# A recurrence split into two stages: RWKV block and cross-attention on one core

## Chip, core, metric

One core of a Trainium2 chip. The metric is the device time of one execution in microseconds (us); the time of a kernel is the median of its runs.

## What is computed

Sixteen sequences x[b] (128 tokens, 512 channels) and as many contexts ctx[b] go through two layers in fp32. The first is an RWKV block: a layer norm, interpolation of each token with the one before it, five mixed inputs, from them r, k, v, gate g and a per-channel decay w, a recurrence over time on 32 heads of 16x16 state, a group norm, an output projection and a gated feed-forward. The state comes from rows of ctx. The second is a cross-attention of the result with the same context.

```python
xa = _ln(x, ln1_w, ln1_b)
sx = concatenate([state[:, 1:2] - xa[:, :1], xa[:, :-1] - xa[:, 1:]], axis=1)
xxx = tanh((xa + sx * maa_x) @ maa_w1).reshape(b, l, 5, DM)
xm = xa[:, :, None] + sx[:, :, None] * (maa_stack + einsum('blfd,fde->blfe', xxx, maa_w2))
xk, xw, xv, xr, xg = (xm[:, :, j] for j in range(5))
w = exp(-exp(time_decay + tanh(xw @ td_w1) @ td_w2))
r, k, v, g = xr @ Wr.T, xk @ Wk.T, xv @ Wv.T, silu(xg @ Wg.T)
def step(s, r_t, k_t, v_t, w_t):            # scanned over 128 tokens
    a = k_t[..., :, None] * v_t[..., None, :]
    out = einsum('bhi,bhij->bhj', r_t, u * a + s)
    return a + w_t[..., :, None] * s, out
...
x1 = x + groupnorm(out) * g @ Wo.T
xc = _ln(x1, ln2_w, ln2_b)
x2 = x1 + sigmoid(xr2 @ Wfr.T) * (square(relu(xk2 @ Wfk.T)) @ Wfv.T)
...
A = softmax(conv(Wn, inorm(x2)).T @ conv(Wm, inorm(ctx)))
return conv(Wo, conv(Wl, ctx) @ A.T) + x2
```

## The kernel before

The sixteen sequences are worked in eight groups g of n = 2 sequences b. A group passes through Python generators, each of which yields after every piece of its work:

- stageB: layer norm and transposes (norm_T, xaT), the shift sx, the product p1 with maa_w1, tanh, and the stacked operand sk (lines 222 to 257).
- stageB2: five interpolations px, xm in the order 0, 3, 1, 2, 4, one ahead of its use; from them k, r, w, v and the gate, in five pieces. v and the gate go to DRAM (vD, gD). w is ready after the third piece.
- stageR: the recurrence, in chunks of 32 tokens. For each sequence, pair products over blocks of four tokens are laid out in PP (L374) from ru = u*r (L371), summed over a head by matmuls with emat into pq (L385), transposed (L390) and put into the attention matrix AM (L392). Then three levels (blocks of 4, 8 and 16 tokens): k is scaled by running decays in place (L416), copied to ks (L401), spread block-diagonally into KX by eight DMAs on SP's queue (L405), multiplied with r (pl, L435) and put into AM (L437). Last, for each sequence: k transposed to kt (L457), the state carried over three chunks (pu L479, Sn, Sx), AM transposed to at (L493), and the output po (L500, L505), its variance and the group norm of y (L524).
- stageC: y transposed (py, L545), gate, Wo (ptk, L559), second layer norm, feed-forward Wfk (L586), Wfr, Wfv.
- stageL: the cross-attention of the group (pn, pS, pA, pO, lines 663 to 688); stageX loads what it needs of the context (MV), which stageE computed earlier into DRAM.

Of the eight PSUM banks bx and c have two each, pt, lv, ls and la one each. A tile waits until its buffer (same tag) is free. The recurrence uses lv (pq, pl, pu, po) and pt (p4, pk, pa); pt also serves the transposes of both layer norms and of y. One buffer each: wl, ru and at (one tag), kt, y, PP, AM, KX, w; two each: k, r, vt, xaT, sx, and the stacked operand stk[g % 2].

A loop over steps sets the order. In a step, stage k of group step - OFF[k] is live (B 0, B2 1, R 2, C 3, L and X 4), and interleave takes the next piece of the stage with the least DLY + share done; NEED says which stage of the same group must be over. EARLY gives the groups whose contexts are computed in steps 0 to 2 as extra work. That order is a priority: when the program is built, a scheduler fills each engine's queue with the instruction of highest priority whose operands and buffers are free in its own model of time. On the chip each queue then runs in order. All loads are issued on SP's queue.

Of the kernel before, what the change touches and what calls it, by code (L numbers as in the profile page):

```python
# [7 lines left out]
FP = mybir.dt.float32  # L8
# [10 lines left out]
n = 2  # L19
# [7 lines left out]
OFF = [0, 1, 2, 3, 4, 4]  # L27
ORDER = [3, 4, 2, 1, 0, 5]
DLY = [-0.2, 0.2, 0.0, 0.4, 0.8, 0.4]
EARLY = {0: [0, 1], 1: [2, 3], 2: [4, 5, 6, 7]}  # L30
LASTX = 2
# [3 lines left out]
def rwkv_xattn_kernel(ctx: ExitStack, tc: tile.TileContext, a: dict, out: bass.AP):  # L35
# [9 lines left out]
    PSB = dict(bx=2, c=2, pt=1, lv=1, ls=1, la=1)  # L45
# [55 lines left out]
    stk = [const.tile([98, 5, 256], FPR, name=f"sk{i}") for i in range(2)]  # L101


    KX = const.tile([128, 4 * n, 8, 64], FP, name="KX")
# [4 lines left out]
    def clear():  # L109
        for sk in stk:  # L110
            nc.gpsimd.memset(sk[96:98].bitcast(FP), 1.0)
        nc.gpsimd.memset(PP.rearrange("p a f -> p (a f)"), 0.0)
        nc.gpsimd.memset(KX.rearrange("p a h s -> p (a h s)"), 0.0)
        nc.gpsimd.memset(VX.rearrange("p c q f -> p (c q f)"), 0.0)
        nc.gpsimd.memset(AM.rearrange("p b h s -> p (b h s)"), 0.0)
# [72 lines left out]
    def norm_T(xs, sidx, vw, vb, g, xT, how, ssum):  # L188
# [7 lines left out]
        for c0 in range(0, 4, 2):  # L196
            pt = ps.tile([128, 2, n, 128], FP, name="pt", **T("pt"))
# [24 lines left out]
    def stageB(g):  # L222
# [3 lines left out]
        xaT = sb.tile([128, 4, n, 129], FP, name="xaT")  # L226
        norm_T(x, 1, V_LN1W, V_LN1B, g, xaT, "dve", (None, None))
        yield
        sx = sb.tile([128, 4, n, 128], FP, name="sx")
# [14 lines left out]
        th = sb.tile([128, 2, NT], FP, name="th", tag="xn")  # L244
# [4 lines left out]
        sk = stk[g % 2]  # L249
# [10 lines left out]
    def stageB2(g):  # L260
        d = D[g]
        xaT, sx, sk = d["xaT"], d["sx"], stk[g % 2]
# [85 lines left out]
    def stageR(g):  # L348
        d = D[g]
        k, r, w, vt = d["k"], d["r"], d["w"], d["vt"]  # L350

        wl = sb1.tile([128, 4 * n, 124], FP, name="wl")
        src = w.rearrange("p c b t -> p (c b) t")
        for m in PRO:
            v = src.rearrange("p a (k s) -> p a k s", s=2)
            dst = wl[:, :, WOFF[2 * m] : WOFF[2 * m] + 64 // m]
            nc.vector.tensor_tensor(dst, v[:, :, :, 0], v[:, :, :, 1], ALU.mult)
            src = dst
        kf, rf = (t.rearrange("p c b t -> p (c b) t") for t in (k, r))
        s0 = sb1.tile([128, n, 4, 16], FP, name="s0")  # L360
        nc.sync.dma_start(out=s0.rearrange("p b c j -> p (b c j)"), in_=a["s0"][g])
        sm = small.tile([128, n, 4], FP, name="sm")
        nc.vector.tensor_reduce(sm, s0, AX.X, ALU.add)
        nc.vector.tensor_scalar(sm, sm, 1.0 / S, None, ALU.mult)
        nc.vector.tensor_tensor(s0, s0, sm[:, :, :, None].to_broadcast([128, n, 4, 16]), ALU.subtract)
# [3 lines left out]
        ru = sb1.tile([128, 4, n, 128], FP, name="ru", tag="at")  # L369
        for cc in range(4):  # L370
            nc.scalar.activation(ru[:, cc], r[:, cc], AF.Identity, scale=vec[:, V_U, cc : cc + 1])  # L371

        def pairs(b):
            tt = lambda o, x, y: nc.vector.tensor_tensor(o, x, y, ALU.mult)  # L374
            tt(dg[:, :, :, 0:128:4], four(ru, b, 0, 4), four(k, b, 0, 4))
# [7 lines left out]
            pq = ps.tile([128, 512], FP, name="pq", **T("lv"))  # L383
            for cc in range(4):
                nc.tensor.matmul(pq[32 * cc : 32 * cc + 32], lhsT=emat, rhs=PP[:, cc, 0:512], start=True, stop=True)  # L385
            pc = sb1.tile([128, 512], FP, name="pc4", tag="kt")
            nc.scalar.copy(pc, pq)
            p4 = ps.tile([128, 4, 4, 32], FP, name="p4", **T("pt"))
# [8 lines left out]
        def expand(li):  # L397

            m = LEV[li]
            ks = sb1.tile([128, 4 * n, 64], FP, name="ks", tag="sq")  # L400
            nc.scalar.copy(ks.rearrange("p a (q m) -> p a q m", m=m),  # L401
                           kf.rearrange("p a (q s m) -> p a q s m", s=2, m=m)[:, :, :, 0])
            for h in range(8):
                p = slice(16 * h, 16 * h + 16)
                nc.sync.dma_start(out=KX[p, :, h], in_=ks[p])  # L405

# [10 lines left out]

        for b in range(n):
            pairs(b)
            yield  # L420
        decay(kf, 1, 0)
        decay(kf, 2, 0)
        expand(0)
        decay(kf, 4, 0)
        decay(rf, 1, 1)
        decay(rf, 2, 1)
        yield
        for li, m in enumerate(LEV):
            pl = []
            for b in range(n):  # L430
                t = ps.tile([128, 512], FP, name="pl", **T("lv"))
                for cc in range(4):
                    for c in range(4):
                        cs = slice(32 * c, 32 * c + 32)
                        nc.tensor.matmul(t[cs, 128 * cc : 128 * cc + 128], lhsT=r[:, cc, b, cs],  # L435
                                         rhs=KX[:, n * cc + b, :, 16 * c : 16 * c + 16], start=True, stop=True)
                nc.vector.copy_predicated(  # L437
                    AM[:, b].rearrange("p h (q s m) -> p h q s m", s=2, m=m)[:, :, :, 0],
                    lvm[:, li].rearrange("p (q m) -> p q m", m=m)[:, None].to_broadcast([128, 32, 16 // m, m]),
                    t.rearrange("p (h q m) -> p h q m", h=32, m=m))  # L440
                yield
            decay(rf, m, 1)
            if li < 2:
                expand(li + 1)
                decay(kf, 2 * m, 0)
            yield
        y = sb1.tile([128, n, 512], FP, name="y")
        var = small.tile([128, n, 32], FP, name="var", bufs=2)
        for b in range(n):
# [4 lines left out]

            pk = ps.tile([128, 512], FP, name="pk", **T("pt"))
            for cc in range(4):
                nc.tensor.transpose(pk[:, 128 * cc : 128 * cc + 128], k[:, cc, b], ident)  # L457
            kt = sb1.tile([128, 512], FP, name="kt")
            nc.scalar.copy(kt, pk)

# [10 lines left out]
            vb = vt[:, b].rearrange("p (q x j) -> p x q j", q=4, x=8)  # L471
            yield
            for c in range(3):
                cs = slice(32 * c, 32 * c + 32)
                pu = ps.tile([128, 4, 4, 16], FP, name="pu", **T("lv"))
                for cc in range(4):
                    for hf in range(2):
                        f = slice(64 * hf, 64 * hf + 64)
                        nc.tensor.matmul(pu[f, cc], lhsT=kt[cs, 128 * cc + 64 * hf : 128 * cc + 64 * hf + 64],  # L479
                                         rhs=vb[cs, 2 * cc + hf], start=True, stop=True)  # L480
                wc = wl.rearrange("p (c b) s -> p c b s", b=n)[:, :, b, WOFF[32] + c]
# [6 lines left out]

            at = sb1.tile([128, 8, 128], FP, name="at")
            for x4 in range(2):  # L490
                pa = ps.tile([128, 4, 128], FP, name="pa", **T("pt"))
                for x in range(4):
                    nc.tensor.transpose(pa[:, x], AM[:, b, 4 * (4 * x4 + x) : 4 * (4 * x4 + x) + 4].rearrange("p h s -> p (h s)"), ident)  # L493
                nc.scalar.copy(at[:, 4 * x4 : 4 * x4 + 4], pa)
            yield
            po = ps.tile([128, 512], FP, name="po", **T("lv"))
            for cc in range(4):
# [4 lines left out]
                for x in (2 * cc, 2 * cc + 1):  # L502
                    for c in range(4):
                        cs = slice(32 * c, 32 * c + 32)
                        nc.tensor.matmul(po[cs, 64 * x : 64 * x + 64], lhsT=at[:, x, cs],  # L505
# [23 lines left out]
    def behind(g):  # L529

        return tc.issue_after(D[g]["last"].ins) if g < G else nullcontext()

    def stageC(g):
        d = D[g]
        with behind(g + 1):
# [6 lines left out]
        for b in range(n):  # L542
            pt = ps.tile([128, 4, 128], FP, name="py", **T("pt"))
# [30 lines left out]
        norm_T(x, 0, V_LN2W, V_LN2B, g, xcT, "act", ssum)  # L574
# [70 lines left out]
    def stageX(g):  # L645
        d = D[g]
        d["MV"] = []
        for b in range(n):
# [4 lines left out]
            with behind(g + 2):  # L653
# [4 lines left out]
    def stageLb(g, b):  # L658
# [5 lines left out]
        pn = ps.tile([128, 512], FP, name="pn", **T("ls", g, ("pt", "bx")[b]))  # L664
# [3 lines left out]
        for tt in range(4):  # L668
            tsl = slice(128 * tt, 128 * tt + 128)
            pS = ps.tile([128, 512], FP, name="pS", **T("ls", g, ("c", "lv")[b]))  # L670
# [135 lines left out]
```

## Time and profile before

| | |
|---|---|
| runs | 1028.33, 1029.72, 1031.13 us; median 1029.72 |
| profiled execution | 1028.91 us, span 1027.1 us |
| mean granted TensorE clock | 0.978 |
| busy | PE 933.8, PE weight loads 633.5, DVE 650.3, ACT 499.8, POOL 66.8 us |
| DMA | 128.7 MB on SP's queue, 41.3% of 16 engines; 33698 of 76461 packets under 512 B |

The page names engines PE (TensorE; PEld its weight loads, which overlap), DVE (VectorE), ACT (ScalarE), POOL (GpSimd) and SP (the queue that issues DMAs). The time of the execution includes 1.8 us around the span. In a line of the timeline or of groups, "out<-in" are tiles, the bracket gives idle time of that engine just before, and what ended it. L12 is line 12 of the kernel before.

### The profile page before, as it was taken

The numbers are of one execution on the slowest core, as the hardware profiler recorded it, in microseconds if no ns is written. First come the engines' busy times: TensorE is split into PE (matmuls) and PEld (weight loads), VectorE is DVE, ScalarE is ACT, GpSimd is POOL, SyncE is SP. The second block draws the span as 40 slices with busy tenths as digits, with TensorE's granted clock in tenths as the row PEclk, the third lists the DMA queues.
The fourth block names the chain that finished last, engine by engine and source line by source line (L and its number), as shares of the span: only waits on it lengthen the run. The fifth ranks groups of instructions, "written<-read, shape, count | busy, mean of one in ns | idle before, by whom it ended". The sixth has DMA issues, their size and how long they took to land.

```text
span 1027.1 us, 19266 instructions
## 1 busy us (share of the span) xinstructions
PE 933.8 (91%) x7588; PEld 633.5 (62%) x7588; DVE 650.3 (63%) x1569; ACT 499.8 (49%) x1017; POOL 66.8 (6%) x92
## 2 busy tenths in 40 slices
PE   4699899769998999999999999899999997897997
PEld 2565766546755586666765685657766664573655
DVE  6777766764757574874686485766594658463423
ACT  2565451253336543574446444464344555534645
POOL 5111000000000000000100000000000000000000
PEclk9899998889998999999999999999999999998999
DMA  5765646314641334515551435414454334262210
GB/s 158 246 219 190 192 134 198 97 26 140 225 134 21 108 122 145 168 18 155 177 176 38 128 112 165 138 32 145 144 174 120 90 127 138 39 193 64 77 57 32
DMA packets 76461, 129.91 MB, mean 126 GB/s; under 512 B 33698, under 2 KB 43426, under 8 KB 76369
## 3 DMA queue, kind: packets, MB, share of 16 engines
q1 hardware_dynamic: 76370, 128.68, 41.3%
q8 instruction: 60, 0.98, 0.4%
q14 instruction: 31, 0.25, 0.1%
HBM read 100.32 MB, written 22.04 MB: 119 GB/s over the span
## 4 chain that ended last, share of the span: by engine, by line
PE 65%; DVE 11%; ACT 9%; DMA 7%; SPq 4%; issue 2%; POOL 0%; ACTq 0%; DVEq 0%; POOLq 0%
PE ptk L559 15%; PE pj L219 13%; PE pj L586 5%; PE pv L321 5%; PE pO L685 4%; PE pS L671 4%; SPq L405 3%; PE pl L435 3%; PE pu L479 3%; PE p L241 2%; DVE PP L374 2%; PE pa L493 2%; DMA KX<-ks 2%; PE po L500 2%; PE pA L680 2%
## 5 line engine op out<-in xcount | busy, mean ns | idle before, releaser
L219 PE MATMUL pj<-xm,wb 128*128 128x256 f32 x768 | 182.7, 388 | 8.4 <-DVE xm L281 4.1
L219 PEld LDWEIGHTS pj<-xm,wb 128*128 128x128 f32 x768 | 145.2, 195 | 36.5 <-issue 8.2
L138 POOL TENSOR_TENSOR rs<-rs,mhalf 128x1 f32<-128x1 f32 x64 | 48.0, 754 | 586.0 <-DVE rs L123 509.7
L685 PEld LDWEIGHTS pO<-AT,MV 128*128 128x128 f32 x448 | 57.2, 191 | 18.5 <-issue 7.8
L671 PE MATMUL pS<-MV,Mn 128*128 128x512 f32 x112 | 59.8, 616 | 6.6 <-ACT e L675 3.7
L685 PE MATMUL pO<-AT,MV 128*128 128x128 f32 x448 | 62.3, 279 | 3.8 <-ACT AT L682 3.8
L281 DVE TENSOR_TENSOR xm<-px,sx 128x512 f32<-128x512 f32 x80 | 54.5, 686 | 14.7 <-PE px L278 14.5
L559 PE MATMUL ptk<-wb,yT 128*128 128x512 f32 x128 | 58.4, 610 | 2.3 <-issue 2.3
L673 DVE TENSOR_REDUCE nm<-pS 128x1 f32<-128x512 f32 x64 | 43.9, 690 | 25.6 <-PE pS L671 25.3
L559 PE MATMUL ptk<-wb,sx 128*128 128x512 f32 x128 | 58.9, 601 | 0.4 <-DMA wb<-in_Wfr_dram 0.3
L435 PE MATMUL pl<-KX,r 128*32 128x128 f32 x1536 | 53.5, 279 | 6.1 <-DMA KX<-ks 5.2
L586 PE MATMUL pj<-xk,wb 128*128 128x256 f32 x256 | 58.2, 380 | 0.3 <-DVE xk L145 0.3
L321 PE MATMUL pv<-wb,xm 128*128 128x512 f32 x128 | 57.5, 594 | 0.1
L559 PE MATMUL ptk<-wb,kk 128*128 128x512 f32 x128 | 57.5, 598 | 0.0
L675 ACT ACTIVATE e<-pS,nm 128x512 f32<-128x512 f32 x64 | 44.9, 701 | 23.5 <-DVE nm L673 23.5
L677 ACT ACTIVATE e<-e,nm 128x512 f32<-128x512 f32 x64 | 46.2, 725 | 19.2 <-DVE nm L676 19.0
L435 PEld LDWEIGHTS pl<-KX,r 128*32 128x32 f32 x1536 | 40.0, 111 | 23.8 <-issue 11.5
L282 DVE TENSOR_TENSOR xm<-xm,xaT 128x512 f32<-128x512 f32 x80 | 54.3, 687 | 0.5
L586 PEld LDWEIGHTS pj<-xk,wb 128*128 128x128 f32 x256 | 47.4, 190 | 6.5 <-DVE xk L145 0.6
L278 PE MATMUL px<-sk,w2s 98*128 98x256 f32 x160 | 42.9, 354 | 7.3 <-ACT w L302 4.9
L437 DVE COPY_PREDICATED AM<-lvm,pl 128x512 f32<-128x512 int32 x48 | 33.8, 705 | 23.4 <-PE pl L435 23.0
L682 ACT COPY AT<-pA 128x512 f32<-128x512 f32 x64 | 37.8, 590 | 19.7 <-PE pA L680 16.8
(160 smaller groups left out, 1685.8 us busy)
## 6 DMA issues: line engine op xcount, KB each, us to landing
mvD<-MVe SPq DMA_DIRECT2D x16, 512.0 KB, 3.8
wb<-in_Wk_dram SPq DMA_DIRECT2D x16, 512.0 KB, 3.5
wb<-in_Wr_dram SPq DMA_DIRECT2D x16, 512.0 KB, 3.9
wb<-wvc SPq DMA_DIRECT2D x16, 512.0 KB, 3.5
wb<-in_Wg_dram SPq DMA_DIRECT2D x16, 512.0 KB, 4.8
wb<-in_Wo_dram SPq DMA_DIRECT2D x16, 512.0 KB, 3.7
wb<-in_Wfk_dram SPq DMA_DIRECT2D x16, 512.0 KB, 4.3
wb<-in_Wfr_dram SPq DMA_DIRECT2D x16, 512.0 KB, 3.8
```

What stands on the lines that cost most here:

```text
L138: D["pow"] = nc.gpsimd.tensor_tensor(rs, rs, mhalf[:, 0:1], ALU.pow).ins
L219: nc.tensor.matmul(pj[:, m], lhsT=wb[:, m, cc, :], rhs=xm[:, cc], start=cc == 0, stop=cc == 3)
L281: nc.vector.tensor_tensor(xm[:, sl], px.rearrange("p c (b t) -> p c b t", b=n), sx[:, sl], ALU.mult)
L282: nc.vector.tensor_tensor(xm[:, sl], xm[:, sl], xaT[:, sl, :, 1:129], ALU.add)
L321: nc.tensor.matmul(pv, lhsT=xm[:, m, b], rhs=wbs[m // 2][:, m % 2], start=m == 0, stop=m == 3)
L435: nc.tensor.matmul(t[cs, 128 * cc : 128 * cc + 128], lhsT=r[:, cc, b, cs], rhs=KX[:, n * cc + b, :, 16 * c : 16 * c + 16], start=True, sto ...
L559: nc.tensor.matmul(pt, lhsT=act[:, m, b], rhs=wbs[m // 2][:, m % 2], start=m == 0, stop=m == 3)
L586: nc.tensor.matmul(pj[:, m], lhsT=wb[:, m, cc, :], rhs=xk2[:, cc], start=cc == 0, stop=cc == 3)
L671: nc.tensor.matmul(pS, lhsT=Mn[:, tsl], rhs=Mm, start=True, stop=True)
L675: nc.scalar.activation(e, pS, AF.Exp, bias=nm[:, 0:1], accum_out=nm[:, 1:2])
L677: nc.scalar.activation(e, e, AF.Identity, scale=nm[:, 2:3])
L685: nc.tensor.matmul(pO, lhsT=Vc[:, sc], rhs=AT[:, sc], start=sc == 0, stop=sc == 3)
```

## The change

stageR becomes stageR1 (pairs, levels, kt and at for both sequences) and stageR2 (state, po, y). R1 has a PSUM bank r1, R2 a bank r2; pt and lv are gone, B's layer-norm transposes use bx, C's use c. kt, at and w32 (the decays that R2 reads) are results of their own. R1 of a group becomes live in the step of its B2 and starts after B2's third piece; R2 and C follow in the next step, L one step later, so a group spans four steps instead of five. WHEN holds, for each stage, step offset, start, length and number of pieces. xaT, sx and the stacked operand have one buffer instead of two. ru is gone: u is applied in place on PP by ACT. KX is laid out with the head outside, and ks is made ahead (expand) of the copies into KX (place).

```diff
-OFF = [0, 1, 2, 3, 4, 4]
-ORDER = [3, 4, 2, 1, 0, 5]
-DLY = [-0.2, 0.2, 0.0, 0.4, 0.8, 0.4]
-EARLY = {0: [0, 1], 1: [2, 3], 2: [4, 5, 6, 7]}
+WHEN = {
+    B_: (0, 0.85, 0.3, 3),
+    B2_: (1, 0.2, 1.0, 5),
+    R1_: (1, 0.75, 0.7, 14),
+    R2_: (2, 0.0, 0.7, 14),
+    C_: (2, 0.8, 1.0, 5),
+    L_: (3, 0.3, 1.0, 6),
+    X_: (3, -0.1, 0.2, 2),
+}
+EARLY = {0: [0, 1], 1: [2, 3, 4], 2: [5, 6, 7]}
...
-    PSB = dict(bx=2, c=2, pt=1, lv=1, ls=1, la=1)
+    PSB = dict(bx=2, c=2, r1=1, r2=1, ls=1, la=1)
...
-    stk = [const.tile([98, 5, 256], FPR, name=f"sk{i}") for i in range(2)]
-    KX = const.tile([128, 4 * n, 8, 64], FP, name="KX")
+    sk = const.tile([98, 5, 256], FPR, name="sk")
+    KX = const.tile([128, 8, 4 * n, 64], FP, name="KX")
...
-            pt = ps.tile([128, 2, n, 128], FP, name="pt", **T("pt"))
+            pt = ps.tile([128, 2, n, 128], FP, name="pt", **T(bank))
...
-        xaT = sb.tile([128, 4, n, 129], FP, name="xaT")
+        xaT = sb1.tile([128, 4, n, 129], FP, name="xaT")
-        sx = sb.tile([128, 4, n, 128], FP, name="sx")
+        sx = sb1.tile([128, 4, n, 128], FP, name="sx")
...
-        ru = sb1.tile([128, 4, n, 128], FP, name="ru", tag="at")
-        for cc in range(4):
-            nc.scalar.activation(ru[:, cc], r[:, cc], AF.Identity, scale=vec[:, V_U, cc : cc + 1])
...
-            tt(dg[:, :, :, 0:128:4], four(ru, b, 0, 4), four(k, b, 0, 4))
+            tt(dg[:, :, :, 0:128:4], four(r, b, 0, 4), four(k, b, 0, 4))
+            for cc in range(4):
+                q = dg[:, cc, :, 0:128:4]
+                nc.scalar.activation(q, q, AF.Identity, scale=vec[:, V_U, cc : cc + 1])
...
-            ks = sb1.tile([128, 4 * n, 64], FP, name="ks", tag="sq")
+            ks = sb.tile([128, 4 * n, 64], FP, name="ks", tag="ks")
...
+        def place(ks):
             for h in range(8):
                 p = slice(16 * h, 16 * h + 16)
-                nc.sync.dma_start(out=KX[p, :, h], in_=ks[p])
+                nc.sync.dma_start(out=KX[p, h], in_=ks[p])
...
+        place(expand(0))
+        decay(kf, 4, 0)
+        k1 = expand(1)
...
+        for b in range(n):
+            level(0, b)
+            yield
+        place(k1)
+        decay(rf, 4, 1)
+        k2 = expand(2)
...
+        kt = d["kt"] = sb1.tile([128, n, 512], FP, name="kt")
+        for b in range(n):
+            pk = ps.tile([128, 512], FP, name="pk", **T("r1"))
...
+        at = d["at"] = sb1.tile([128, n, 8, 128], FP, name="at")
...
+    def stageR2(g):
+        d = D[g]
+        r, kt, at, w32 = d["r"], d["kt"], d["at"], d["w32"]
...
-                pu = ps.tile([128, 4, 4, 16], FP, name="pu", **T("lv"))
+                pu = ps.tile([128, 4, 4, 16], FP, name="pu", **T("r2"))
...
-            po = ps.tile([128, 512], FP, name="po", **T("lv"))
+            po = ps.tile([128, 512], FP, name="po", **T("r2"))
...
-            pt = ps.tile([128, 4, 128], FP, name="py", **T("pt"))
+            pt = ps.tile([128, 4, 128], FP, name="py", **T("c"))
...
+    NEED = {B_: (), B2_: (B_,), R1_: (), R2_: (R1_, B2_), C_: (R2_,), L_: (C_, X_), X_: (), E_: ()}
+    def ready(k, g):
+        return all((q, g) in done for q in NEED[k]) and (k != R1_ or count.get((B2_, g), 0) >= 3)
```

## The prediction

> **What bounds the kernel now.** I read the page first: busy time and chain.
>
> ```profile
> PE 933.8 (91%) x7588; PEld 633.5 (62%) x7588; DVE 650.3 (63%) x1569; ACT 499.8 (49%) x1017; POOL 66.8 (6%) x92
> ...
> PE 65%; DVE 11%; ACT 9%; DMA 7%; SPq 4%; issue 2%; POOL 0%; ACTq 0%; DVEq 0%; POOLq 0%
> ```
>
> TensorE is the bound, with 1027.1 - 933.8 = 93.3 us without a matmul. The change neither removes nor adds a matmul, so all it can touch is where those 93.3 us lie. The view by windows, cut where the stages of the pipeline change, says where (first number after the window: its length; then PE busy):
>
> ```profile
> 0.00:80.00 80.00, 54.77 (x262) 39.99 (x262) 54.02 (x150) 40.93 (x79) 24.64 (x30) 0.94 0.65 209
> 80.00:230.00 150.00, 127.56 (x1135) 91.55 (x1136) 102.82 (x231) 61.40 (x129) 6.99 (x11) 0.94 0.46 138
> 230.00:776.00 546.00, 527.30 (x4447) 358.95 (x4446) 369.09 (x873) 268.91 (x554) 26.59 (x37) 0.99 0.42 127
> 776.00:935.00 159.00, 147.49 (x1419) 95.81 (x1417) 91.91 (x227) 76.77 (x153) 4.87 (x8) 1.00 0.41 117
> 935.00:1027.10 92.10, 76.70 (x328) 47.16 (x328) 32.51 (x91) 51.76 (x106) 3.67 (x6) 0.96 0.16 52
> ```
>
> PE's idle time is 25.2 us in the first 80 (loading, before any recurrence), 22.4 to 230 (pipeline filling), 18.7 to 776 (five steady steps, 96.6% busy), 11.5 to 935 and 15.4 to the end (draining). So the steady part has 3.4% to give, and the fill and the drain the rest.
>
> Third view, the timeline round the hand-over from group 1's recurrence to group 2's, to see what holds it:
>
> ```profile
> 285.62 0.68 PE L479 MATMUL pu<-vt,kt 32*64 32x64 f32 x16
> ...
> 294.02 0.41 PE L505 MATMUL po<-VX,at 128*32 128x64 f32 x16
> 295.23 1.71 ACT L371 ACTIVATE ru<-r,vec 128x256 f32<-128x256 f32 x4
> 297.06 1.13 DVE L374 TENSOR_TENSOR PP<-ru,k 128x512 f32<-128x512 f32 x1
> 302.30 1.07 PE L385 MATMUL pq<-PP,emat 128*32 128x512 f32 x8
> 310.59 1.93 PE L385 MATMUL pq<-PP,emat 128*32 128x512 f32 x8 [4.26 <-DVE PP L374]
> ```
>
> ru shares at's buffer, so ru(2) waits for the last po(1) at 294.4, although r, k and w of group 2 exist; and PE then waits 4.26 us for the pair products. The same stands at 202.02 in the fill (4.86 us for PP), at 205.6 (1.6 us, a transpose of L200 waiting for AM L392: one bank, pt) and at 224.10 (1.45 us, py waiting for the copy of kt: pt again). From pq to the last po the one recurrence takes 194.7 to 294.4, then 302.3 to 405, 412.8 to 514: 100 to 103 us of a period of 110 to 115 (first Wo matmuls at 349.4, 459.7, 572.6, 687.3). It is a serial chain nearly as long as the period, and in the fill (C of group 0 can't start before y at 196, and starts at 224) it is longer than what PE has beside it.
>
> **The change, part by part.** The profiled run is 1028.9 us (span 1027.1 and 1.8 round it), 0.8 below the median 1029.7; I count from it.
>
> *Two stages, own banks and results.* R1 (pairs, three levels, kt, at) of a group no longer waits for the group before: its buffers are free once that group's R1 is over, kt and at excepted, which R2 must have read. R2's chain is short: in the drain pu(7) starts at 900.0, po of the first sequence ends at 907.3, y is scaled at 937.5, 38 us with C(6) beside. Fill: of the 22.4 us, I can name 11.8 as waits in R's own chain (1.95 at 104, 0.71+4.86+0.75+1.62+0.46 from 196 to 209, 1.45 at 222); beyond these, C(0), 32 us of matmuls, comes a step earlier, into the thin stretch 195 to 230. I take 14 and leave 8, the rate at which 135 to 175 idles now. Steady: of 18.7 I take 6 (4.26 and the 0.77 at 257.8 are R's, the rest is spread over exponentials, loads and softmax waits, which stay). Drain to 935: of 11.5 I take 4 (KX and PP waits of 1.27, 0.82 and 1.10 us, and something for the rest of R). End: y(7) and C(7) come earlier, while C(6) and L(6) still have work; of 15.4 I take 5, the waits of 2.79 and 2.28 us for y and yT. L(7) alone, from 996, keeps its 7 us. Sum: 14+6+4+5 = 29. Bounds: 12 (only the waits named outright in the fill) to 44 (everything after 80 us at the 1% idle of a quiet stretch, 855 x 1% = 9 left, plus the 15.4 at the end: 93 - 25 - 9 - 15).
>
> *Pair products scaled in place.* Four ru activations a group go, eight on strided quarters come, between the first product and pq.
>
> ```profile
> L371 ACT ACTIVATE ru<-r,vec 128x256 f32<-128x256 f32 x32 | 13.8, 501 | 0.1
> L547 ACT ACTIVATE yT<-py,vec 128x128 f32<-128x128 f32 x64 | 24.5, 489 | 7.1 <-PE py L545 7.1
> L374 DVE TENSOR_TENSOR PP<-ru,k 128x512 f32<-128x512 f32 x16 | 17.8, 1112 | 12.4 <-ACT ru L371 9.2 <-PE pq L385 3.3
> ```
>
> From below 0.28 us each (dt, 128x128, 278 ns); from above 0.79 (0.489 times 1112/690, what the stride of four costs on DVE). I take 0.49, the row of that shape with a scale: 8 x 0.49 - 4 x 0.50 = +1.9 us of ACT per group, hidden under ACT's 51% idle. In the chain it is 2.0 us per sequence, under the other five products (2.9 us of DVE) if those don't wait for it. Uncovered it shows for group 0 and group 7 alone: -2 (ru's 1.7 us ahead of the chain are gone) to +8; I take +2.
>
> *KX turned, so that a head's rows are 2 KB in one piece.* A train of eight copies stands before each level:
>
> ```profile
> KX<-ks SPq DMA_DIRECT2D x192, 32.0 KB, 2.2
> ...
> L405 SPq DMA_DIRECT2D KX<-ks x192: 585/598/1193, 99.4 to 886.8; - x192
> ...
> L654 SPq DMA_DIRECT2D MV<-mvD x14: 320/327/707, 256.9 to 904.9; - x14
> ```
>
> Issue: 598 ns against 327 for a plain two-dimensional copy: 8 x 0.27 = 2.2 us a level, 6.5 a group; landing 2.2, at best the 1.9 of s0's load (64 KB in 512 B pieces). On the path only where R1 leads (groups 0 and 7): 0 to -14, inside the 29. The moving operand now steps 2 KB between heads; no row shows it. I take nothing, with -0 to +0.3 us for each 1.08 us level (48 of them, +14) as bounds. [...] The row of s0, in pieces of 512 B, allows no more than 0.3 us a level.
>
> *Moved or shared.* B's transposes go from pt to bx (24 uses per group of two banks where 22 were), C's to c (12 for 8). Each such use is held for two transposes' worth and its evacuation, 1 to 2 us; PE is in order, so a late bank stops all matmuls behind it. 0 to 4 us in all, I take 1. R1 puts all 16 fills on one bank, pq(b=1) now behind the AM copies of b=0 (1.45 us); DVE's next products take 4 us anyway: nothing. place() waits on SP for the level before to be read; Wfv, Wo and MV loads queue behind it, as they do now (88.8 us of SP waits on pl): nothing. EARLY moves one group's context from step 2 to step 1: the same 37 us of filler.
>
> *xaT, sx and sk single.* B(g+1) may write only when B2(g) has its last xm. From the last xm to the next px there are now 18.7, 16.3, 21.5, 23.9, 28.7, 22.8 and 23.2 us; from the first xaT to the last sk of a group 14.7 to 17.8 us from group 3 on, 25 and 32 in the fill. It fits, narrowly. The new wait falls on an ACT instruction (L203) and a DVE one (sx); behind them on those queues stand the evacuations of pj, pS and pA, and PE waits for these. 0 to +8, I take +1 with the fill's other work as cover; the price without cover is the first rival.
>
> Sum: 1028.9 - 29 + 2 + 1 + 1 = 1003.9, so **1004 us**.
>
> [...]
>
> **The rivals.** *The B loop becomes the bound (slower).* B2 spreads its interpolations over 87.5 us in a steady step (256.0 to 343.5). If B's chain, now strictly behind it, takes the 32 us it once took (110.2 to 142.1), the loop is 119.5 against 112: 5 steps x 7.5 = 37, less 21 gained at both ends: 1045. It decides from a B chain of 24.5 us. Against: B2 has been done in 45 us (107.4 to 152.7), so it can be squeezed. Chance 0.20.
> *They don't run beside each other.* R1(g+1) starts only after B2's third piece, when w is there (343.5 for group 3); if R2 is then over, what is left is the freed banks and the shorter drain, about 14: 1015. Chance 0.10.
> *R was never in the way.* The waits move to y, to loads and softmax: 1029 within 3. The even 96.6% speaks for it, the 4.26 and 4.86 us against. Chance 0.06.
> *All of it comes:* 985, the 44 above. Chance 0.14.
>
> **How the numbers follow.** My case, 992 to 1016, has 0.50. Faster is it and the 1015 and 985 cases: 0.74; same 0.06; slower 0.20. A measurement of this kernel tells 0.3%, 3 us, from no change. The range 985 to 1045 leaves out half of the 985 case and half of the slow one, some 0.17.
>
> **What would show it.** Right: pq of a group before the last po of the group before; the first Wo near 205 instead of 237; PE idle in 80 to 230 under 10 us; KX issues near 0.33 us. Wrong: px of a group over 30 us behind the last xm of the one before; PE waiting for ACT at L203 or for sk; a first Wo later than 237; a period over 115.

## The result, and the profile after

The kernel after takes 1038.1 us (median; 1031.49 to 1044.6) where before, on the same chips, took 1030.93: a ratio of 1.0057, interval 1.0034 to 1.0079. It is slower by 6 us by this ratio (7 by the medians), where 26 less had been forecast. The profiled execution of after took 1035.88 us, with a span of 1034.1 (before: 1028.91 and 1027.1).

Busy times and the chain that ended last, of after, from its page:

```profile
PE 953.9 (92%) x7588; PEld 643.7 (62%) x7588; DVE 644.6 (62%) x1569; ACT 509.2 (49%) x1049; POOL 61.9 (6%) x91
...
PE 71%; DVE 11%; DMA 8%; ACT 6%; issue 2%; SPq 1%; POOL 0%; ACTq 0%; DVEq 0%; POOLq 0%
```

TensorE without a matmul fell from 93.3 to 1034.1 - 953.9 = 80.2 us, about half of what was forecast. But the same 7588 matmuls now keep it busy for 20.1 us more. In the chain, the shares of ACT (9 to 6%) and of SP's queue (4 to 1%) shrank, and PE itself grew by as much (65 to 71%). The windows, cut as in the prediction:

```profile
0.00:80.00 80.00, 54.50 (x254) 38.39 (x255) 53.09 (x139) 38.08 (x71) 20.42 (x28) 0.98 0.63 207
80.00:230.00 150.00, 134.68 (x1216) 97.28 (x1215) 105.28 (x252) 65.84 (x134) 9.02 (x14) 0.97 0.51 164
230.00:776.00 546.00, 532.61 (x4349) 356.55 (x4348) 354.80 (x859) 283.28 (x597) 25.84 (x37) 0.98 0.37 117
776.00:935.00 159.00, 151.68 (x1339) 101.28 (x1337) 95.34 (x218) 71.50 (x147) 4.43 (x8) 0.99 0.40 128
935.00:1034.10 99.10, 80.41 (x436) 50.18 (x436) 36.11 (x103) 50.51 (x102) 2.19 (x4) 0.94 0.13 43
```

The idle time is 25.5, 15.3, 13.4, 7.3 and 18.7 us (before 25.2, 22.4, 18.7, 11.5, 15.4). Up to 935 there is less idle time, as forecast. Yet in the steady window PE is 97.5% busy and does fewer matmuls (4349 against 4447). Where do busy microseconds go that do no more work? The timeline of PE in after, round an output po (first number the start, then the time of the group; x is its count; L with a number is a line of that kernel):

```profile
238.18 0.60 PE L478 MATMUL pa<-ident,AM 128*128 128x128 f32 x4
238.71 0.42 PE L530 MATMUL po<-Sx,r 128*32 128x128 f32 x8
239.07 3.70 PE L589 MATMUL ptk<-wb,kk 128*128 128x512 f32 x8
...
243.96 0.66 PE L478 MATMUL pa<-ident,AM 128*128 128x128 f32 x4
244.45 3.60 PE L589 MATMUL ptk<-wb,kk 128*128 128x512 f32 x8
247.98 0.43 PE L535 MATMUL po<-VX,at 128*32 128x64 f32 x16
248.23 0.38 PE L530 MATMUL po<-Sx,r 128*32 128x128 f32 x2
248.54 0.66 PE L478 MATMUL pa<-ident,AM 128*128 128x128 f32 x4
```

po opens its bank at 238.71 with the eight products of Sx, while at, its other operand, is only half transposed (the second pa comes at 243.96); the products with at follow at 247.98, are cut once more by the next sequence's pa, and the bank is held until 251. The 96 matmuls of a po, which took 1.75 to 1.83 us in one piece in 10 of 16 cases before, take 2.7 to 12.5 us here, with 3 to 48 other matmuls between them.

For what follows I split the span of a profiled run four ways, from the start times of its matmuls (a matmul's time runs to the start of the next one, less idle time):

- *idle*: the span less PE's busy time;
- *small*: pu, po and pl, the recurrence's products on 32 rows or columns, at whatever clock;
- *half*: what all other matmuls lose where the granted clock is recorded as 0.5, that is half of their time there (in before the matmuls pj start every 216 ns at 1.0 and every 427 at 0.5, in after pO every 112 and 213);
- *rest*: the span less these three, the other matmuls at full clock.

Two of the ten runs of banks_late were in the slow state of a lower clock (0.967 and 0.968, the others 0.972 to 0.985) and are left out. The span and the four parts belong to the one profiled execution, which can lie some microseconds from the median (b_late 8 above, banks_late 7 below).

| kernel | median us | ratio to before, interval | span | idle | small | half | rest |
|---|---|---|---|---|---|---|---|
| before | 1030.9 | | 1027.1 | 93.3 | 112.1 | 17.3 | 804.4 |
| after | 1038.1 | 1.0057 [1.0034, 1.0079] | 1034.1 | 80.2 | 126.2 | 17.1 | 810.6 |
| gate | 1065.3 | 1.0297 [1.0246, 1.0347] | 1067.0 | 88.1 | 134.8 | 32.0 | 812.1 |
| b_sooner | 1061.3 | 1.0232 [1.0167, 1.0296] | 1060.4 | 87.1 | 130.6 | 30.9 | 811.8 |
| nudge | 1048.3 | 1.0145 [1.0117, 1.0172] | 1048.5 | 85.6 | 130.3 | 24.7 | 807.9 |
| po_order | 1040.3 | 1.0088 [1.0055, 1.0122] | 1037.6 | 84.7 | 125.2 | 11.2 | 816.5 |
| vx_first | 1045.2 | 1.0116 [1.0070, 1.0162] | 1046.6 | 84.4 | 127.8 | 22.4 | 812.0 |
| one_bank | 1151.3 | 1.1132 [1.1068, 1.1196] | 1149.3 | 149.8 | 126.2 | 56.0 | 817.3 |
| b_kx | 1032.9 | 1.0004 [0.9976, 1.0032] | 1030.4 | 93.2 | 113.9 | 19.0 | 804.3 |
| b_late | 1050.6 | 1.0187 [1.0131, 1.0242] | 1057.2 | 102.5 | 119.0 | 31.4 | 804.3 |
| diag | 1028.1 | 0.9948 [0.9918, 0.9977] | 1027.7 | 89.9 | 114.3 | 20.5 | 803.0 |
| banks | 1012.8 | 0.9823 [0.9746, 0.9900] | 1010.2 | 80.8 | 112.4 | 13.5 | 803.5 |
| banks_5 (the same) | 1014.8 | 0.9812 [0.9777, 0.9847] | 1013.2 | 81.4 | 113.4 | 16.2 | 802.2 |
| banks_late | 1027.5 | 0.9938 [0.9896, 0.9980] | 1018.4 | 79.7 | 114.8 | 14.1 | 809.8 |
| banks_at | 1036.5 | 1.0024 [1.0002, 1.0046] | 1034.5 | 87.0 | 118.6 | 23.3 | 805.6 |
| at_back | 1033.4 | 1.0010 [0.9984, 1.0037] | 1027.2 | 83.8 | 122.7 | 12.6 | 808.1 |
| early_b | 1072.7 | 1.0374 [1.0319, 1.0428] | 1072.6 | 104.9 | 127.1 | 30.9 | 809.7 |
| all_back | 1072.5 | 1.0417 [1.0380, 1.0455] | 1070.2 | 107.9 | 127.6 | 28.2 | 806.5 |

After against before: idle -13.1, small +14.1, half -0.2, rest +6.2: +7.0, the difference of the spans. Of the 126.2 us of small matmuls 11.5 ran at half clock, of before's 112.1 only 1.8, and there they lose nearly half of their time too (a matmul of pl takes 26.6 ns at 1.0 and 49.7 at 0.5 in after, of po 19.1 and 36.3, of pu 32.2 and 52.1); so, as an estimate, about 5 of the 14.1 us are clock in this pair of executions. By tile, po takes 9.0 of them, pu 3.2 and pl 2.0. Of the rest, 3.6 us are the matmuls of p1 (at 19 to 25 us thirteen of them take 427 ns or more instead of 216, before five) and 3.5 those of pw. Those of p1 look like clock too: the record of the clock begins at 25.85 us (before at 22.95), and from there on they take 216 ns.

The clock can also be followed over all executions, since each has its span and its mean granted clock. Span x (1 - clock) is an estimate of what the lower clock took. As a mean over the executions of a kernel it is 27 to 28 us for before, 25 for after, 31 for nudge, 36 and 37 for b_sooner and gate, 41 for b_late, 76 for one_bank, 22 to 24 for banks, 34 for banks_at, 23 for banks_late and 20 for at_back. So the clock does not explain why after is slower than before; of several differences below it is a large part.

### The profile page after: what moved, and what is told of

Its sections match the earlier page's. It is cut to its first block, busy times and chain, and to the rows that moved or that the text cites. A ratio compares the mean times of both kernels' runs of the same rounds, so it can differ in the third digit from the quotient of the medians.

```text
span 1034.1 us, 19263 instructions
## 1 busy us (share of the span) xinstructions
PE 953.9 (92%) x7588; PEld 643.7 (62%) x7588; DVE 644.6 (62%) x1569; ACT 509.2 (49%) x1049; POOL 61.9 (6%) x91
## 4 chain that ended last, share of the span: by engine, by line
PE 71%; DVE 11%; DMA 8%; ACT 6%; issue 2%; SPq 1%; POOL 0%; ACTq 0%; DVEq 0%; POOLq 0%
PE ptk L589 15%; PE pj L225 13%; PE pv L326 5%; PE pO L715 5%; PE pj L616 5%; PE pS L701 4%; PE pl L428 4%; PE pA L710 2%; PE po L530 2%; PE po L535 2%; PE p L247 2%; DMA xs<-in_ctx_dram 2%; PE pu L517 1%; PE px L283 1%; PE pn L695 1%
## 5 line engine op out<-in xcount | busy, mean ns | idle before, releaser
L225 PEld LDWEIGHTS pj<-xm,wb 128*128 128x128 f32 x768 | 142.4, 191 | 40.5 <-issue 17.4
L144 POOL TENSOR_TENSOR rs<-rs,mhalf 128x1 f32<-128x1 f32 x64 | 39.1, 616 | 704.3 <-DVE rs L129 668.2
L715 PE MATMUL pO<-AT,MV 128*128 128x128 f32 x448 | 65.8, 293 | 6.7 <-ACT AT L712 6.7
L428 PE MATMUL pl<-KX,r 128*32 128x128 f32 x1536 | 55.6, 280 | 8.2 <-DVE AM L430 4.0
L707 ACT ACTIVATE e<-e,nm 128x512 f32<-128x512 f32 x64 | 46.5, 730 | 28.2 <-DVE nm L706 28.2
L716 DVE SCALAR_TENSOR_TENSOR x<-pO,cb,x 128x128 f32<-128x128 f32 x64 | 22.2, 347 | 42.5 <-PE pO L715 42.1
```

Of the source, the lines that this page charges most:

```text
L225: nc.tensor.matmul(pj[:, m], lhsT=wb[:, m, cc, :], rhs=xm[:, cc], start=cc == 0, stop=cc == 3)
L707: nc.scalar.activation(e, e, AF.Identity, scale=nm[:, 2:3])
L715: nc.tensor.matmul(pO, lhsT=Vc[:, sc], rhs=AT[:, sc], start=sc == 0, stop=sc == 3)
```

## The experiments

**First guesses: one wait, one order, one time.** Four kernels on the base of after.

*gate*: the gate leaves the one buffer it shares with xq, the operand of p1.

```
-            gt = sb1.tile([128, 4, n, 128], FP, name="gt", tag="gt")
+            gt = sb.tile([128, 4, n, 128], FP, name="gt", tag="xm")
```

> The changed kernel, but the gate's tile gt takes a buffer of xm, so that xq and thhl of the next group no longer wait for the gate's write to DRAM. Loop theory: in the changed kernel xq starts 3 to 7 us after every gate write and px 16 to 24 us after that, so that px(7) comes at 797 us (706 before) and the last group's chain behind it is late; here xq follows xaT at once, px(7) comes at 740 or earlier, and the time falls by 15 to 30 us, below 1020. Efficiency theory (TensorE is 97% busy between 230 and 776 us, so the loop is hidden, and the 20 us of extra busy time are the loss): px(7) may come earlier, the time falls by less than 5 us. Reshuffle theory (any edit rearranges all queues, and the 6 us are of that size): the time moves by 5 us either way.

*po_order*: the last chunk of Sx first.

```
-                for c in range(4):
+                for c in (3, 0, 1, 2):
```

> The changed kernel, but the chunk that is ready last (c = 3) goes first in po, so that po starts only when all four states are there. In the changed kernel po is cut in pieces and takes 4 to 12 us with 20 to 48 foreign matmuls between, where it took 1.75 us in one piece before. Efficiency theory: po is whole again in most of 16 cases, busy time of TensorE falls by 5 us or more, and the time by 5 to 8 us. Loop theory: the time stays within 4 us. Reshuffle theory: 5 us either way without a link to busy time.

*b_sooner*: stage B at 0.75 of the step instead of 0.85.

```
-    B_: (0, 0.85, 0.3, 3),
+    B_: (0, 0.75, 0.3, 3),
```

> The changed kernel with stage B's start at 0.75 instead of 0.85, which puts xq (0.95) ahead of the gate (1.0) in priority, so that xq may take the shared buffer first. Loop theory: where it does, px of the next group comes 15 us or more sooner, px(7) before 760 us, and the time falls by 10 us or more, unless the gate's projection then holds a PSUM bank. Efficiency theory: within 5 us. Reshuffle theory: 5 us either way.

*nudge*: the last stage at 0.33 instead of 0.30.

```
-    L_: (3, 0.3, 1.0, 6),
+    L_: (3, 0.33, 1.0, 6),
```

> The changed kernel with stage L's start at 0.33 instead of 0.30: nothing that any theory names. It is a yardstick for what a mere reordering of the queues does. Loop and efficiency theories: within 3 us. Reshuffle theory: 4 to 8 us away.

Measured: 1065.3, 1040.3, 1061.3 and 1048.3 us. In gate the wait of xq for the gate's write (10.3 us in four places of after) is gone, but the interpolations of group 7 start at 794.7 instead of 797.4, and the time is 27 us longer: that wait wasn't what made them late. b_sooner, meant to bring B forward, makes the gate later (its writes come 16 to 40 us later) and moves the interpolations of group 7 to 807.8. By gate the theory of a loop through the gate falls. po_order leaves po cut up (3.0 to 13.6 us) and small at 125, so it didn't test what it was made for. nudge, which is meant to add or remove no wait, costs 10 us, 6 of them clock by the estimate above: a new order of the queues alone can do that here, and a difference of a few microseconds between two orders isn't yet a cause.

**One part of the change undone, or done alone.**

*one_bank*: pu and po back in the bank of the first stage; one of the eight banks stays empty.

```
-                pu = ps.tile([128, 4, 4, 16], FP, name="pu", **T("r2"))
+                pu = ps.tile([128, 4, 4, 16], FP, name="pu", **T("r1"))
...
-            po = ps.tile([128, 512], FP, name="po", **T("r2"))
+            po = ps.tile([128, 512], FP, name="po", **T("r1"))
```

> After with pu and po in the bank of R1 (one PSUM bank for the recurrence, one of eight left empty), so that R2 of a group and R1 of the next can't interleave their fills freely. If work beside each other is what the kernel lives from, 1050 or more, and the fill idles over 20 us in 80 to 230. If the order of the queues alone sets the time and the second bank is worth little, within 10 us of after, 1030 to 1048.

*b_late*: before, with B behind the interpolations (in group 0 as it was).

```
-DLY = [-0.2, 0.2, 0.0, 0.4, 0.8, 0.4]
+DLY = [0.8, 0.2, 0.0, 0.4, 0.8, 0.4]
...
```

> Before with stage B begun at 0.8 of the step instead of -0.2, that is behind the interpolations as in after; nothing else. Theory of the late B (the interpolations of the next group come late, and that alone costs what the split gained): 1040 to 1050, last xm to next px over 35 us. Theory that only the order as a whole counts (each new order has its own half-clock stretches and hidden waits): anywhere from 1025 to 1045, with the gap as long.

*b_kx*: before, with KX turned.

```
-    KX = const.tile([128, 4 * n, 8, 64], FP, name="KX")
+    KX = const.tile([128, 8, 4 * n, 64], FP, name="KX")
...
-                nc.sync.dma_start(out=KX[p, :, h], in_=ks[p])
+                nc.sync.dma_start(out=KX[p, h], in_=ks[p])
...
-                                         rhs=KX[:, n * cc + b, :, 16 * c : 16 * c + 16], start=True, stop=True)
+                                         rhs=KX[:, :, n * cc + b, 16 * c : 16 * c + 16], start=True, stop=True)
```

> Before with KX turned (a head's rows in one piece of 2 KB), nothing else. By the sum of the prediction 0 to -14 us, nearest -2: 1018 to 1030. If the moving operand's stride of 2 KB costs, pl's start-to-start time rises above 48 us in all. If a new order alone moves the time by up to 10 us, 1020 to 1040 with neither of these to see.

*vx_first*: after, with VX's products opening the sum of po and those of Sx added (the first write of a bank's parts changes hands with it, and po's sum is another).

```
-                                     rhs=Sx[:, c, cc].rearrange("p h j -> p (h j)"), start=True, stop=True)
+                                     rhs=Sx[:, c, cc].rearrange("p h j -> p (h j)"), start=False, stop=True,
+                                     skip_group_check=True)
...
-                                         rhs=VX[:, c, :, 16 * x : 16 * x + 16], start=False, stop=True,
-                                         skip_group_check=True)
+                                         rhs=VX[:, c, :, 16 * x : 16 * x + 16], start=True, stop=True)
```

> After with the two kinds of po matmuls in the other order (VX's product starts the sum, Sx's is added), so that po begins only when its last operand, VX, has landed. Theory of the cut-up po (its 96 matmuls take 1.75 us in one piece, 2.7 to 12.5 us with 3 to 48 others between them): po in fewer pieces, PE busy under 946, 1028 to 1033. Theory of the order as a whole: po in fewer pieces, the time anywhere from 1030 to 1050, going with the half-clock stretches.

Measured: one_bank 1151.3, so the second bank carries over 110 us of the kernel after, 52 of them clock by the estimate above (the fill idles 17.9 us, not over 20). What the second bank lets start early is the same group's state: pu of group 3 begins at 434, beside its own levels (pl to 471); in one_bank it begins at 558, behind the last pa. b_late 1050.6, 19 us over before: standing behind the interpolations costs before idle time (102.5) and clock (31.4; 14 us more than before by the estimate over all executions). b_kx 1032.9, no difference, though the orders of its queues differ much from before's: a new order may also cost nothing. In vx_first po is in fewer pieces (2.0 to 8.5 us, 0 to 24 others between), but small stays at 128, PE is busy for 962 us instead of under 946, and the time rises by 7 instead of falling: po in somewhat fewer pieces was worth nothing there.

**The parts put together on the base of before.**

*diag*: before with the pair products scaled in place, the last decays in a tile w32 of their own, and KX turned.

```
-        ru = sb1.tile([128, 4, n, 128], FP, name="ru", tag="at")
...
-            tt(dg[:, :, :, 0:128:4], four(ru, b, 0, 4), four(k, b, 0, 4))
+            tt(dg[:, :, :, 0:128:4], four(r, b, 0, 4), four(k, b, 0, 4))
+            for cc in range(4):
+                q = dg[:, cc, :, 0:128:4]
+                nc.scalar.activation(q, q, AF.Identity, scale=vec[:, V_U, cc : cc + 1])
...
```

> Before with the pair products scaled in place (no ru, so no wait of the next group's pairs for at), the last decays in a tile of their own (w32) and KX turned; banks, stages and B as before. If the wait of ru for at (4.26 and 4.86 us at two hand-overs) was worth its size at each hand-over: 1005 to 1020. If the waits only move, since pq then waits for the bank of po and p4 for that of pa: 1025 to 1035.

*banks*: diag, and the banks of after: pq, p4 and pl in r1; pk, pu, pa and po in r2; the norms' transposes in bx and c, py in c. The recurrence stays one stage, at and kt are made per sequence, xaT, sx and the stacked operand keep two buffers.

```
-    PSB = dict(bx=2, c=2, pt=1, lv=1, ls=1, la=1)
+    PSB = dict(bx=2, c=2, r1=1, r2=1, ls=1, la=1)
...
```

> The same as diag, and the recurrence's PSUM banks dealt as in after: one for pq, p4 and pl, one for pk, pu, pa and po, the transposes of the norms and of y in bx and c. The most of the change that keeps two buffers of xaT, sx and sk. If own banks bring the two halves beside each other: PE idle in 230 to 776 under 15 us and 1005 to 1020. If more fills on bx, c and the first bank take it back: 1030 to 1045.

*early_b*: after, with B at its old place and two buffers for its results.

```
-    B_: (0, 0.85, 0.3, 3),
+    B_: (0, -0.2, 1.0, 3),
...
-        xaT = sb1.tile([128, 4, n, 129], FP, name="xaT")
+        xaT = sb.tile([128, 4, n, 129], FP, name="xaT")
...
-        at = d["at"] = sb1.tile([128, n, 8, 128], FP, name="at")
+        at = d["at"] = sb1.tile([128, 1, 8, 128], FP, name="at")
...
```

> After with stage B back at its old place (-0.2 of the step, beside the interpolations of the group before), for which xaT, sx and the stacked operand have two buffers again. To make room, AM, kt and at hold one sequence that is used for both, so the recurrence's result is left wrong, at the same instructions. Theory that the split is worth what was forecast and that the single xaT, sx and sk, which put B behind the last interpolation, took it away (b_late: 19 us): 1008 to 1022, last xm to next px under 30 us, PE busy under 945. Theory that any new order costs half-clock time and hidden waits: 1030 to 1050 with the gap just as short.

Measured: diag 1028.1, 5 us under before: the waits of ru for at were worth little by themselves. pq of a group still starts 4 to 8 us behind the last po of the one before, with which it shares a bank. banks 1012.8 and, run again, 1014.8: 18 to 20 us under before. It beats both kernels. Two of its windows, and one po from its timeline:

```profile
80.00:230.00 150.00, 137.13 (x1121) 97.27 (x1120) 113.49 (x266) 73.79 (x159) 8.05 (x14) 0.95 0.46 144
230.00:776.00 546.00, 527.83 (x4522) 364.14 (x4521) 365.09 (x864) 275.40 (x571) 18.42 (x35) 0.99 0.40 128
```

```profile
366.93 0.42 PE L501 MATMUL po<-Sx,r 128*32 128x128 f32 x8
367.18 0.41 PE L506 MATMUL po<-VX,at 128*32 128x64 f32 x16
367.40 0.40 PE L501 MATMUL po<-Sx,r 128*32 128x128 f32 x8
```

Against before it wins 12.5 us of idle time, 9.5 of them in the window of the fill (12.9 against 22.4); the steady window idles 18.2 us, not under 15 as expected. Yet the recurrences of two groups do run beside each other: pq of a group starts 26 to 46 us ahead of the last po of the one before, and the steps are 109.0 us apart (Wo of groups 1 to 5), before 113.3.

The idle time of banks, 80.8 us, is that of after; it is 24 us faster all the same, by small (112.4), half and rest. In banks po stands behind pa in one bank, can't open it before at is there, and runs in one piece in 14 of 16 cases. The steady window holds 4522 matmuls where after's holds 4349. And the interpolations of a group begin 18 to 52 us behind the last one of the group before, in after 38 to 63: the mark I had set for trouble stands in the fastest kernel too.

early_b fell: 1072.7, 35 us over after. From the last xm to the next px there are 17 to 88 us, not under 30, so its theory wasn't put to the test. B early in the order of after meets something else. SP's queue, there, with the load of the next x (xn):

```profile
217.97 2.07 SPq L217 DMA_DIRECT2D wb<-in_Wfk_dram  x2
220.76 4.94 SPq L411 DMA_DIRECT2D KX<-ks  x8
225.81 0.99 SPq L75 DMA_DIRECT2D xn<-in_x_dram  x2
```

x of group 3 is issued behind the first stage's last placement, at 225.8; its transposes come at 240.9 and use bx; and px of group 2, whose operand is complete at 155, takes bx after them, at 249.2 (in after 192.1).

**Which of the steps between banks and after costs.** Between them lie at and kt made ahead in the first stage, B behind the interpolations with single xaT, sx and sk, the order in two stages, and smaller edits (ks made ahead, EARLY).

*at_back*: after, with at in the second stage again, per sequence, before po and in its bank.

```
-        at = d["at"] = sb1.tile([128, n, 8, 128], FP, name="at")
...
-                pa = ps.tile([128, 4, 128], FP, name="pa", **T("r1"))
...
+            at = sb1.tile([128, 8, 128], FP, name="at")
+            for x4 in range(2):
+                pa = ps.tile([128, 4, 128], FP, name="pa", **T("r2"))
```

> After with at taken back to where it stood: its transposes in the second stage, one sequence at a time, just before po and in po's bank; kt, the two stages, their banks and the single xaT, sx and sk stay. Theory that at, being ready early, lets po begin before its other operands are there and be cut up (small matmuls of the recurrence, po, pu and pl, take 112 us in before, 126 in after, 112 in banks): po in one piece of 1.75 us in most of 16 cases, those matmuls under 116 us, 1015 to 1028. Theory that B behind the interpolations is what costs: po in one piece too, perhaps, but 1035 to 1045.

*banks_late*: banks with the edit of b_late.

> The kernel banks (1012.8 us) with stage B begun at 0.8 of the step, behind the interpolations, as in b_late. If B's place is what costs: about 19 us more, as in b_late, 1025 to 1038. If it costs only where waits of the recurrence stand beside it: 1010 to 1020. Small matmuls of the recurrence stay near 112 us by either.

*all_back*: at_back, kt moved back likewise, two buffers for xaT and sx, B at -0.2. With one stacked operand and B ahead, a group's interpolations read the next group's operand, and px waits for that B; its 1072.5 us, as in early_b, tell of that order and not of the causes asked for.

> After with at and kt both taken back to the second stage, one sequence at a time; the room goes to a second buffer for xaT and sx (th lies in the buffer of xn again), and B is begun at -0.2 of the step. The stages, their banks and the single sk stay. If the two causes (po cut up, B late) are what stands between after and banks: 1008 to 1020. If B's early place is bad in this order of stages, as in early_b (1072.67): over 1040, with po in one piece all the same.

*banks_5* and *banks_at*, on one chip: banks, and banks with at of both sequences made ahead, in the first bank; AM holds one sequence, which is used for both.

```
-    AM = const.tile([128, n, 32, 32], FP, name="AM")
+    AM = const.tile([128, 1, 32, 32], FP, name="AM")
...
+        at = sb1.tile([128, n, 8, 128], FP, name="at")
+        for b in range(n):
+            for x4 in range(2):
+                pa = ps.tile([128, 4, 128], FP, name="pa", **T("r1"))
...
-                pa = ps.tile([128, 4, 128], FP, name="pa", **T("r2"))
```

> The kernel banks once more, as the yardstick for banks_at on one chip and for a narrower interval: 1008 to 1018, ratio 0.975 to 0.988.

> The kernel banks with at made ahead for both sequences, its transposes in the first bank, before the state's chain, as in after. To make room AM holds one sequence that is used for both, so the recurrence's result is left wrong, at the same instructions. Theory of the cut-up po (at_back: 1033 against 1038): po no longer in one piece, po, pu and pl together over 120 us instead of 112, 5 to 12 us above banks. Theory that at ahead costs nothing by itself: within 3 us of banks.

Measured: banks_at 1036.5 against 1014.8, +21.6 us by at made ahead (with the room for it, AM for one sequence, in the same edit). Its timeline shows how: po opens between two pa, and its next operand comes 8 us later.

```profile
369.08 0.60 PE L453 MATMUL pa<-ident,AM 128*128 128x128 f32 x4
369.61 0.43 PE L502 MATMUL po<-Sx,r 128*32 128x128 f32 x8
376.95 0.60 PE L453 MATMUL pa<-ident,AM 128*128 128x128 f32 x4
377.48 0.43 PE L507 MATMUL po<-VX,at 128*32 128x64 f32 x16
```

By the four parts it is small +5.2, half +7.1, idle +5.6, rest +3.4 (spans 1034.5 and 1013.2). So the cut-up po is shown, but the recurrence's products are a quarter of the price, a little less than expected (118.6 us, not over 120); the rest comes with the shifted order: pu waits 6.4 us for the state Sn instead of 0.7, and the clock is halved more often (34 us against 22 by the estimate over all executions, so 12 of the 21.6). banks_late is 1027.5, 13 to 15 over banks, with executions from 1015.8 to 1030.9. at_back gets 1033.4, 5 under after (forecast by that theory: 1015 to 1028). By the estimate these 5 us are all clock (20 against 25), so of the theory's gain nothing else came: po of a group's first sequence is whole again in all eight cases, that of the second still takes 5 to 6 us in five of eight, and small stays at 122.7.

So either step alone, put into banks, takes 13 to 22 of the 23 to 25 us that lie between banks and after; both together don't take the sum, and undoing at in after returns only 5. What the order in two stages costs by itself was not isolated.

The traces do show what became of the overlap. Hand-over from group 4 to group 5 in after (w is the decay that the pair products need):

```profile
615.30 2.16 ACT L307 ACTIVATE w<-pw,vec 128x128 f32<-128x128 f32 x8
617.91 1.11 ACT L308 ACTIVATE w<-w 128x1024 f32<-128x1024 f32 x1
...
622.91 0.31 PE L535 MATMUL po<-VX,at 128*32 128x64 f32 x4
...
631.51 1.06 PE L386 MATMUL pq<-PP,emat 128*32 128x512 f32 x8
```

pq of group 5 starts 8.5 us behind the last po of group 4, as in before (7.5 to 8.9). Of the seven hand-overs only the first has pq clearly ahead (14 us); two are level, four have it 1 to 9 us behind. In after w is ready 8 to 15 us before pq starts, in before from group 2 on 65 to 77, in banks 44 to 58. So the first stage no longer waits for the group before, but for w, which comes late in the order of after. The late place of B alone doesn't bring that about: in banks_late w stands 33 to 46 us ahead from group 2 on.

## Why the prediction was wrong, point by point

*All it can touch is where those 93.3 us lie.* This step failed. I took PE's busy time as fixed, since no matmul came or went, and since sixteen Wo matmuls of before run 7.06 us without a hole (from 459.98). The same 7588 matmuls took 929.4 us (banks) to 999.5 (one_bank). In after they took 20 more than before, and that is more than the 13 of idle time that were won. That row held for wide matmuls at full clock only: at half clock those of pj in before start every 427 ns instead of 216. In place of fixed busy time the runs show that the order sets it: small products +14.1 us, the rest +6.2.

*Fill 14, steady 6, drain 4, end 5.* Measured 7.1, 5.3, 4.2 and -3.3. In the fill the prediction left 8 us as the rate of 135 to 175; that stretch idles 4.8 us in 40, which is 18 in 150, and 15.3 stayed. The two middle terms were right in size. In part this is luck: pq's waits for its pair products (10.0 us of PE's idle time before) are gone, but pu and po wait 8.8 us for the state, before 0.1. The output projection of group 0 starts at 192.7, even earlier than the 205 I named, but 80 to 230 still idles 15.3 us, not under 10. At the end the sign was wrong: I had y(7) and C(7) earlier, but the last group's interpolations start at 797.4 instead of 706.4 and its Wo at 961 instead of 945.

*The split runs beside the group before.* This step failed too, from the second hand-over on. pq of group 1 does run before the last po of group 0 (timeline of after):

```profile
162.96 0.68 PE L517 MATMUL pu<-vt,kt 32*64 32x64 f32 x16
163.57 1.07 PE L386 MATMUL pq<-PP,emat 128*32 128x512 f32 x8
...
177.37 0.68 PE L535 MATMUL po<-VX,at 128*32 128x64 f32 x15
```

The sign that I had set for being right stands there, and there alone. The rival "They don't run beside each other" had named the reason, w from the third piece of the interpolations, and its condition came true at most hand-overs; its price of 1015 did not, since it too counted idle time alone.

*Scaled in place: 0.49 us each.* Measured 535 ns, and hidden: diag, which has it, isn't slower.

*KX.* I expected issues of 0.33 us. They take 587 ns (before 598), so the train of eight is no shorter; the landing went from 2.2 to 2.0, as the row of s0 (1.9) had allowed. b_kx shows no gain. The moving operand's stride shows no cost in after: pl's mean is 280 ns, before 279 (in b_kx 283).

```profile
L409 SPq DMA_DIRECT2D KX<-ks x192: 507/587/1272, 102.2 to 913.8; - x192
```

*Banks moved: 1 us.* No run prices this by itself; banks moves the norms' transposes and py in the same way and gains on the whole.

*Single xaT, sx, sk: 1 us.* Mis-sized, as far as the stand-ins tell: B behind the interpolations, with two buffers kept, is 13 to 15 us in banks_late and 19 in b_late; in after itself it wasn't undone with success. I had measured whether the chain of B fits into the gap; it does, and the period of the steady steps hardly changed (114.1 us between the Wo of groups 1 and 5, before 113.3). So the rival of 1045 us had the sign but not the mechanism: PE is 97.5% busy in these steps, and no loop became the bound. In b_late the price of the late B is paid in idle time and clock.

*Kept out of the sum: at and kt.* The prediction named them only as results of the first stage that the second must have read. That their bank and place changed was not priced, and banks_at shows 21.6 us for at alone.

## What to carry to other kernels

When a list of instructions is interleaved by priority, an accumulation should not be able to open its PSUM bank before its last operand is near: with the step that makes that operand in the same bank just ahead of it, the accumulation ran in one piece in 14 of 16 cases, and giving this up cost 21.6 us (undoing it in another order returned 5). When a chain is cut in two so that the halves overlap, look for what the first half of the next group waits on then; here it was w. Idle time of the bound engine is only half of an account; look at whether its busy time is the same work at the same clock. And of a change with several parts, the cheapest one alone (here the dealing of banks, on top of diag's small edits, without the second stage and without the buffers it costs) is worth a run of its own: with diag's 0.5% it gave 2% where the whole gave -0.6%.

## What the runs showed of the hardware

The granted clock fell to half (0.50) in stretches of 3.4, 6.8 and 10.2 us, five times longer ones (to 17.1 us) in the 18 traces (3.413, 6.827 and 10.240 in the records of before and after, but for the last stretch of each, which the end of the record cuts). One of them in after, by windows of 3.4 us on the grid of these stretches (after the length: PE's busy time; the last but two is the granted clock):

```profile
367.18:370.60 3.42, 3.42 (x46) 2.37 (x46) 2.63 (x8) 1.47 (x5) 0.55 (x1) 1.00 0.15 42
370.60:374.01 3.41, 1.96 (x32) 1.07 (x27) 3.19 (x11) 2.86 (x10) 0.00 (x0) 1.00 0.01 2
374.01:380.84 6.83, 6.83 (x54) 3.56 (x55) 5.34 (x11) 3.31 (x7) 0.00 (x0) 0.50 0.00 0
```

PE was 57% busy in the 3.4 us ahead of it, and its longest wait there was 1.35 us (pu for Sn); then the clock was halved for two such windows, in both of which PE was busy throughout. On this grid, from the first entry of the clock's record on, the 18 traces have 5025 windows at full clock, and 205 of them were followed by half clock: none of the 4039 in which PE was busy for 0.9 or more, 174 of the 288 in which it was busy for under 0.6. Small products alone don't seem to bring the fall: of 123 windows in which PE was busy for over 0.8, but under 0.2 with the products of the dense layers and the attention (ptk, pj, px, pv, p1, pn, pm, pS, pO, pV), none was followed by it. They go with its lasting: of windows at half clock with PE busy for over 0.9, another followed in 1 of 113 where these products filled over 0.8, and in 33 of 109 where they filled less. Few of the falls came after a window that was nearly idle: 9 of the 205 followed one with PE busy for under 0.05. These are counts over kernels that are much alike; nothing was changed to try them.

The queues ran in the order in which they had been filled. Put together by output tile, the matmuls of PE in the trace of before are 734 stretches, the work of DVE 1214, that of ACT 580, the copies of SP 224, and all of them stand in the order of the built program. A bank that came late shows there as a wait of the whole of PE: 1.62 us ahead of 207.44 (pt, until AM was written) and 1.45 us ahead of 224.10 (py, until kt was copied).
